# Quarter products inside the second block product of a layernorm, attention and mixture-of-experts kernel

## The chip, the cores and the metric

The kernel runs on one core of one Trainium2 chip. The metric is the device time of one execution in microseconds. The program has five engines that run their own instruction queues in order and meet at semaphores: TensorE (PE, matrix products into PSUM banks), VectorE (DVE), ScalarE (ACT), GpSimd (POOL), and SyncE (SP), which here only issues transfers. POOL and ACT issue some transfers too.

## The reference

All arithmetic is in float32. The input x has 4 rows of 1024 tokens of 1024 channels.

```
xn    = layernorm(x)                                  # over the channels
q, v  = xn @ Wq, xn @ Wv
s_t   = sigmoid(beta) * s_(t-1) + v_t                 # along the tokens, per channel
y     = layernorm(q * s) * ln_g + ln_b
attn  = (y * silu(xn @ Wg)) @ Wo
moe   = for each token the top 8 of 64 experts by softmax(xn @ router.T),
        weights normed over the 8; an expert takes at most 128 tokens:
        (silu(t @ w1.T) * (t @ v1.T)) @ w2
out   = x + attn + moe
```

The change touches only the products with Wv, Wq and Wg, and the norming and turning of the tokens that feed them.

## The kernel before, in words

**Stages.** `attn_and_routing` works through the rows b = 0 to 3 one after the other. In a row the products with Wv and Wq alternate (v unit 0, q unit 0, v unit 1 and so on to q unit 3), then come four gate units with Wg. A unit m makes output channels 128 m to 128 m + 127 and the same 512 further, for all 1024 tokens of the row. Then `Experts` runs the experts and the product with Wo to the end. The experts start at about 1215.9 us of the profile.

**A unit.** A unit is one call of `product`: a product of 2 x 2 blocks in the Winograd form of Strassen's method, with seven block products instead of eight. The left blocks are 512 x 128 pieces of a weight matrix (and sums of them), the right blocks B11, B21, B12, B22 are the normed, transposed tokens (512 channels x 512 tokens) and the sums T1 to T4 of them. `steps` writes the order: slot 0 with B11, slot 1 with B21, slot 5 with T2, slot 4 with T1, slot 3 with T3, slot 6 with B22, slot 2 with T4. The inner function `acc` issues one block product as four matmuls of 128 x 128 by 128 x 512 (L145). Bank "a" gathers slots 0, 5, 3 and 2, bank "b" slot 1, bank "c" slots 4 and 6. In between ACT copies banks to SBUF (L156), and DVE adds them to the results c11 (L168), c22 (L177) and c12 (L180). The seventh product of a unit is left over as `before` and is issued inside the next unit, between its second and third. `late` is a hook for work issued behind the fifth.

**Weights and sums.** `left_sums` makes the four left sums of a unit's weights. In row 0 `weights` loads four pieces of 256 KB through SP, POOL adds (L55 to L58), and a store keeps the 1792 KB in `wsum` (L585); later rows load them from there in one transfer. `right_sums`, called by `sums`, makes T3, T1 (in place of B12), T2 and T4 on DVE (L65, L69, L72, L75).

**Tokens.** Row 0's tokens are normed and turned in `prep_first`; `store` writes them to the DRAM table `rows` (L478, POOL's queue). For row b + 1, `prep(b + 1, h)` takes half of the tokens h in two groups of two 128-token tiles: loads through SP, moments on DVE (L293), root on ACT, reciprocal and norm on DVE (L297), and stores to `rows` through POOL (L441). `load_turned` reads them back through SP in 32-row strips (16 transfers of 128 KB a half), and DVE turns them by 32 x 32 squares into the blocks (L462). The tiles x of two groups have one buffer each. `prep` of the first half is called behind q unit 1, `load_turned` behind q unit 2; of the second half before gate 0 and before gate 3.

**Routing.** `scored` makes the router's logits on TensorE (L487), `route` the choice of eight per token on DVE with the exponent on ACT, and stores to `wtab` (L530). `take` keeps each expert's 128 tokens by 16 rounds of MAX8 (L562) and MATCH_REPLACE (L564) on DVE, spread over the units 0 to 3. `find_spread`, the `late` work of gate 0, makes mean and variance of y by matmuls (L620) and the reciprocal root (L695).

**Order.** The program's order on an engine comes from the scheduler, which keeps dependencies and otherwise places by its own estimates; an instruction given to `keep_in_program_order` stays behind those given before it on its engine. An engine that waits for a semaphore holds everything behind it.

Of the kernel before, what the change touches and what calls it, by code (L numbers as in the profile page):

```python
# [9 lines left out]
F32 = mybir.dt.float32  # L10
I32 = mybir.dt.int32
AF = mybir.ActivationFunctionType
# [5 lines left out]
P = 128  # L18
# [23 lines left out]

NSLOT = 7
NWT = 4

# [33 lines left out]
def load_block(nc, to, w, i, c0, n):  # L79

    nc.sync.dma_start(
        out=to, in_=w[i * SH : (i + 1) * SH, c0 : c0 + n].rearrange("(k p) n -> p k n", p=P)
    )
# [22 lines left out]
class Pools:  # L106
# [17 lines left out]

    def x(self, name):
        return self.three.tile([P, 3, S], F32, tag="x", bufs=2, name=name)

# [9 lines left out]

def steps(nc, pools, lhs, blocks, c11, c12, c22, then, name, begun=None):

    def acc(ps, slot, right, start, stop):
        for k in range(KH):
            nc.tensor.matmul(  # L145
                ps,
                lhsT=lhs[:, slot, k, :],
                rhs=blocks[right][:, k, :],
                start=start and k == 0,
                stop=stop and k == KH - 1,  # L150
                skip_group_check=True,
            )

    def copied(ps, part):
        t = pools.scratch.tile([P, SH], F32, tag="sc", name=f"sc{part}_{name}")
        nc.scalar.copy(t, ps)  # L156
        return t

    a, b = begun if begun else (pools.bank("a", [P, SH], f"pa_{name}"), None)
    if not begun:  # L160
        acc(a, 0, "B11", True, True)
    s1 = copied(a, 1)
    yield
    if not begun:
        b = pools.bank("b", [P, SH], f"pb_{name}")
        acc(b, 1, "B21", True, True)
    yield
    nc.vector.tensor_tensor(c11, b, s1, ALU.add)  # L168
    acc(a, 5, "T2", False, True)
    s2 = copied(a, 2)  # L170
    yield
    c = pools.bank("c", [P, SH], f"pc_{name}")
    acc(c, 4, "T1", True, True)
    s5 = copied(c, 5)
    yield
    acc(a, 3, "T3", False, True)
    nc.vector.tensor_tensor(c22, a, s5, ALU.add)  # L177
    yield
    acc(c, 6, "B22", False, True)
    nc.vector.tensor_tensor(c12, c, s2, ALU.add)  # L180
    yield
    acc(a, 2, "T4", False, True)
    then(a)


def product(nc, pools, lhs, blocks, c11, c12, c22, then, before, name, late=None, begun=None):


    todo = steps(nc, pools, lhs, blocks, c11, c12, c22, then, name, begun)
    next(todo)  # L190
    next(todo)
    if before is not None:
        before()
    for _ in range(3):
        next(todo)
    if late is not None:
        late()
    next(todo)
    return lambda: next(todo, None)
# [3 lines left out]
def kernel(  # L203
# [22 lines left out]
    gated = dram.tile([B, NM, P, 4, KH, P], F32, name="gated")  # L226
    wsum = dram.tile([3, NM, P, NSLOT, KH, P], F32, name="wsum")

    pools = Pools(ctx, tc)
# [4 lines left out]
    attn_and_routing(  # L234
        tc, pools, ident, rows, wtab, gated, wsum, x, (wv, wq, wg), beta, ln_g, ln_b, router, out,
        experts.begin, experts.turn_first,
# [3 lines left out]

def attn_and_routing(
    tc, pools, ident, rows, wtab, gated, wsum, x, wvqg, beta, ln_g, ln_b, router, out, routed,
    turn_first
):
# [68 lines left out]
    def prep_first():  # L313
# [3 lines left out]
        for h in range(2):  # L317
            for i in range(2):
                blocks[f"B{i + 1}{h + 1}"] = pools.block(f"xT_0_{h}_{i}")
        groups = [(pools.y if g > 1 else pools.x)(f"x_0_{g}") for g in range(NM)]  # L320
        tiles = [xs[:, j, :] for xs in groups for j in range(2)]
# [90 lines left out]

    stored = {}

    def prep(b, h):

        groups = stored[b, h] = []
        for g in range(NM // 2):

            xs = pools.x(f"x_{b}_{h}_{g}")  # L420
            mv = small.tile([P, 2, 2], F32, tag="mv", name=f"mv_{b}_{h}_{g}")
            r0 = b * S + h * SH + 2 * g * P
            for j in range(2):
                loaded = nc.sync.dma_start(
                    out=xs[:, j, :], in_=x[r0 + j * P : r0 + (j + 1) * P, :]
                )
                tc.keep_in_program_order(loaded)
                moments(xs[:, j, :], mv[:, j, :], f"{b}_{h}_{g}_{j}")
            rs = small.tile([P, 2], F32, tag="rs", name=f"rs_{b}_{h}_{g}")
            nc.scalar.activation(rs, mv[:, :, 1], AF.Sqrt, bias=eps)  # L430
            nc.vector.reciprocal(rs, rs)
            groups.append((r0, xs, mv, rs))
        for r0, xs, mv, rs in groups:
            for j in range(2):

                to = xs[:, (2, 0)[j], :]
                normed(
                    by_quarter(xs[:, j, :], "k q"), mv[:, j, :], rs[:, j : j + 1],
                    by_quarter(to, "q k"),
                )  # L440
                nc.gpsimd.dma_start(out=rows[r0 + j * P : r0 + (j + 1) * P, :], in_=to)  # L441

    def load_turned(b, h):
# [3 lines left out]
        for i in range(2):  # L447
            blocks[f"B{i + 1}{h + 1}"] = pools.block(f"xT_{b}_{h}_{i}")
        for r0, xs, _, _ in stored[b, h]:
            for j in range(2):  # L450
                from_ = rows[r0 + j * P : r0 + (j + 1) * P, :]
                for q in range(NQ):
                    loaded = nc.sync.dma_start(
                        out=xs[q * Q : (q + 1) * Q, j + 1, :].rearrange("i (r c) -> i r c", r=NQ),
                        in_=from_[:, q * DQ : (q + 1) * DQ].rearrange("(r i) c -> i r c", i=Q),
                    )
                    tc.keep_in_program_order(loaded)
        for g, (_, xs, _, _) in enumerate(stored.pop((b, h))):
            for j in range(2):
                n = 2 * g + j  # L460
                for i in range(2):
                    nc.vector.transpose(  # L462
                        blocks[f"B{i + 1}{h + 1}"][:, :, n * P : (n + 1) * P].rearrange(
                            "p k (r i) -> p k r i", i=Q
                        ),
                        xs[:, j + 1, :].rearrange("p (r k j) -> p k r j", r=NQ, j=Q)[
                            :, i * KH : (i + 1) * KH
                        ],
                    )
# [98 lines left out]
    def sums(b):  # L568
        for _ in right_sums(
# [4 lines left out]
        ):  # L574
            pass

    def weights(b, w, m):
# [8 lines left out]
        else:  # L586
            nc.sync.dma_start(out=t, in_=wsum[w, m])
        return t
# [7 lines left out]
    def batch_row(b, left):  # L596
# [11 lines left out]
        spread = []  # L608
        waiting = []

        def collect_waiting():
# [22 lines left out]
        def states(m, left):  # L634

            lo = line.tile([P, S], F32, tag="line", name=f"lo_{b}_{m}")
            hi = line.tile([P, S], F32, tag="line", name=f"hi_{b}_{m}")

            def then(c21):
                scan(lo, lo, m, 0.0)  # L640
                scan(hi[:, H0], c21, m + KH, 0.0)
                scan(hi[:, H1], hi[:, H1], m + KH, hi[:, SH - 1 : SH])

            left = product(
                nc, pools, weights(b, 0, m), quarters[b],
                lo[:, H0], lo[:, H1], hi[:, H1], then, left, f"v_{b}_{m}", collect_waiting,
                begun.get(0) if b == 0 and m == 0 else None,
            )
            return lo, hi, left

        def queries(m, lo, hi, left):
# [12 lines left out]
            def then(c21):  # L664
# [6 lines left out]
                if m == NM - 1:  # L671
                    collect_waiting()

            left = product(
                nc, pools, weights(b, 1, m), quarters[b],
                y(m, H0), y(m, H1), y(m + KH, H1), then, left, f"q_{b}_{m}", None,
                begun.get(1) if b == 0 and m == 0 else None,
            )
            return left
# [18 lines left out]
        def gates(m, w, left):  # L698
            lo = line.tile([P, S], F32, tag="line", name=f"glo_{b}_{m}")
            hi = line.tile([P, S], F32, tag="line", name=f"ghi_{b}_{m}")  # L700

            def then(c21):
# [4 lines left out]
                for i, (c, gate) in enumerate(((m, lo), (m + KH, hi))):  # L707
# [9 lines left out]
                    for h in range(2):  # L717
# [4 lines left out]
                        )  # L722

            return product(
                nc, pools, w, quarters[b],
                lo[:, H0], lo[:, H1], hi[:, H1], then, left, f"g_{b}_{m}",
                find_spread if m == 0 else None,
            )

        taking = take(b)  # L730
        for m in range(NM):
# [15 lines left out]
            if b + 1 < B:  # L747
                if m == 1:
                    prep(b + 1, 0)
                elif m == 2:  # L750
                    load_turned(b + 1, 0)
# [9 lines left out]
        for m in range(NM):  # L761
            if m == 0 and b + 1 < B:
                prep(b + 1, 1)
            if m == NM - 1 and b + 1 < B:
                load_turned(b + 1, 1)
                logits[b + 1] = by_token(b + 1, scored(b + 1))
                sums(b + 1)
            w = weights(b, 2, m)
            if m == NM - 1 and b == B - 1:
# [79 lines left out]
class Experts:  # L849
# [8 lines left out]
    def load(self, e, n):  # L858
# [13 lines left out]
        if slot not in self.slots:  # L872
            t = (pools.x if e == 0 and n < 2 else pools.y)(f"w{n}_{e}")
            self.slots[slot] = t.rearrange("p a b -> p (a b)")
# [422 lines left out]
```

## Time and profile before

| | us |
|---|---|
| median of 3 runs (lowest, highest) | 2531.57 (2531.47, 2532.62) |
| the profiled execution | 2531.94 |
| its span in the profile | 2530.2 |

| stretch of the span, us | what | PE busy | DVE busy | POOL busy |
|---|---|---|---|---|
| 0 to 215.09 | row 0, v and q | 211.55 | 154.44 | 75.24 |
| 215.09 to 322.12 | row 0, gates | 106.51 | 79.23 | 38.49 |
| 322.12 to 1215.9 | rows 1 to 3 | 893.76 | 558.33 | 145.96 |
| 1215.9 to 2530.2 | experts, output | 1305.63 | 937.03 | 506.50 |

The second table comes from the profile's view by stretches. The page gives busy time for each engine; a float32 matmul leaves two records in it and in the timelines. In the timelines a row has its start, its length, engine, line and operation, the tiles written and read, the number of records, and in brackets how long the engine had been idle and what ended that. In the waits a row has the total, the count and the longest. Lines L... are those of the kernel before.

### The profile page before, as it was taken

The page shows a single profiled execution, that of the slowest core. Times are in us where ns is not written, and L with a number is a line of the kernel's source. Part 1 is how long each engine was busy: PE and PEld are TensorE (multiplying, and loading weights), DVE is VectorE, ACT ScalarE, POOL GpSimd, SP SyncE. Part 2 cuts the span into 40 slices and gives each one's busy share as a digit, 9 for nine tenths or more (in the row PEclk, how much of TensorE's full clock was granted, in tenths as well). Part 3 has the DMA queues.
Part 4 walks back from the last instruction along what each step waited for, and adds up shares of the span by engine and source line. Part 5 has one row for each costly group of instructions (what it writes and reads, how often), then busy time and mean ns, then how long its engine had stood idle before and what let it go on. Part 6 is the DMA issues. An engine that isn't in the chain of part 4 may idle for free. (4 is left out here: it accounts for less than half of the span.)

```text
span 2530.2 us, 23616 instructions
## 1 busy us (share of the span) xinstructions
PE 2517.4 (99%) x8253; PEld 1107.4 (44%) x8253; DVE 1729.0 (68%) x2178; ACT 821.7 (32%) x1930; POOL 766.2 (30%) x629
## 2 busy tenths in 40 slices
PE   9999999999999999999999999999999999999998
PEld 5444444444444444444444444444444444444443
DVE  7857659474684747447786767677676768677674
ACT  3112211131111311022253535444454545444452
POOL 0453301201122010231342434344433434344421
PEclk9999999999999999999999999999999999999999
DMA  5665625543344532145799999999999999999995
GB/s 187 256 199 206 203 80 180 186 142 108 133 154 178 166 142 91 59 172 182 279 350 290 309 315 322 311 297 323 308 321 295 313 311 324 309 300 318 312 319 138
DMA packets 122503, 593.80 MB, mean 235 GB/s; under 512 B 15872, under 2 KB 52736, under 8 KB 89360
## 3 DMA queue, kind: packets, MB, share of 16 engines
q1 hardware_dynamic: 81776, 449.08, 48.2%
q0 software_dynamic: 40176, 143.20, 22.0%
q8 instruction: 65, 1.06, 0.2%
q14 instruction: 54, 0.44, 0.0%
q10 hardware_dynamic: 432, 0.01, 0.0%
HBM read 484.19 MB, written 124.81 MB: 241 GB/s over the span
## 5 line engine op out<-in xcount | busy, mean ns | idle before, releaser
L889 POOL DMA_INDIRECT xg<-rows,tables x256 | 290.7, 1136 | 299.0 <-DVE xgT L937 218.7
L976 DVE TENSOR_TENSOR t<-w 128x1536 f32<-128x1536 f32 x128 | 224.3, 1752 | 225.5 <-PE hC L995 222.2
L1087 POOL DMA_INDIRECT out_dram<-ys,tables x64 | 124.5, 1945 | 384.3 <-issue 139.3
L145 PE MATMUL pa_g<-xT,w 128*128 128x512 f32 x512 | 230.9, 594 | 0.5 <-ACT sc_g L156 0.5
L145 PE MATMUL pa_q<-xT,w 128*128 128x512 f32 x480 | 216.4, 593 | 0.0
L145 PE MATMUL pa_v<-xT,w 128*128 128x512 f32 x480 | 215.8, 592 | 0.0
L995 PE MATMUL hC<-t,s 128*64 128x384 f32 x512 | 177.3, 489 | 0.0
L995 PE MATMUL hC<-w,s 128*64 128x384 f32 x512 | 177.3, 490 | 0.0
L1083 PE MATMUL hD<-w,act 128*128 128x512 f32 x384 | 175.3, 592 | 0.6 <-ACT act L1072 0.6
L995 PE MATMUL hA<-w,s 128*64 128x384 f32 x512 | 175.6, 486 | 0.0
L995 PE MATMUL hB<-w,xgT 128*64 128x384 f32 x512 | 175.6, 486 | 0.0
L995 PE MATMUL hA<-w,xgT 128*64 128x384 f32 x512 | 175.6, 486 | 0.0
L995 PE MATMUL hD<-t,s 128*64 128x384 f32 x512 | 175.6, 486 | 0.0
L1083 PE MATMUL hT<-w,act 128*128 128x512 f32 x384 | 175.3, 592 | 0.0
L145 PE MATMUL pa_o<-wo_T,gated 128*128 128x512 f32 x384 | 174.2, 596 | 0.0
L145 PEld LDWEIGHTS pa_g<-xT,w 128*128 128x128 f32 x512 | 96.3, 190 | 123.7 <-issue 123.4
L145 PEld LDWEIGHTS pa_q<-xT,w 128*128 128x128 f32 x480 | 91.1, 190 | 114.5 <-issue 113.0
L145 PEld LDWEIGHTS pa_v<-xT,w 128*128 128x128 f32 x480 | 90.9, 190 | 112.8 <-issue 111.9
L719 POOL DMA_DIRECT2D gated<-y x64 | 48.0, 756 | 302.0 <-DVE y L714 287.7
L1061 ACT COPY act<-s 32x96 f32<-32x96 f32 x480 | 129.0, 269 | 7.0
L1061 ACT COPY act<-t 32x96 f32<-32x96 f32 x480 | 128.9, 269 | 6.0
L145 PE MATMUL pc_g<-xT,w 128*128 128x512 f32 x256 | 115.5, 594 | 0.0
(250 smaller groups left out, 4437.2 us busy)
## 6 DMA issues: line engine op xcount, KB each, us to landing
w<-in_w_dram SPq DMA_DIRECT2D x128, 1536.0 KB, 8.2
w<-in_v_dram SPq DMA_DIRECT2D x64, 1536.0 KB, 8.7
w<-wsum SPq DMA_DIRECT2D x36, 1792.0 KB, 7.4
wsum<-w POOLq DMA_DIRECT2D x12, 1792.0 KB, 6.2
x<-in_x_dram SPq DMA_DIRECT2D x32, 512.0 KB, 9.3
rows<-x POOLq DMA_DIRECT2D x32, 512.0 KB, 4.3
gated<-y POOLq DMA_DIRECT2D x64, 256.0 KB, 5.4
gated<-gated SPq DMA_DIRECT2D x16, 1024.0 KB, 8.4
```

Source lines behind the costliest of these rows:

```text
L145: nc.tensor.matmul(ps, lhsT=lhs[:, slot, k, :], rhs=blocks[right][:, k, :], start=start and k == 0, stop=stop and k == KH - 1, skip_group_ ...
L719: nc.gpsimd.dma_start(out=gated[b, :, :, slot, m, :].rearrange("u p j -> p u j"), in_=yc[:, h * SH : (h + 1) * SH].rearrange("p (u j) -> p ...
L889: nc.gpsimd.indirect_dma_start(out=self.xg[:, e % 2 * NQ + r, :], out_offset=None, in_=self.rows.rearrange("n (q c) -> (n q) c", q=NQ), in ...
L976: self.nc.vector.tensor_tensor(to, a, b, ALU.subtract)
L995: nc.tensor.matmul(bank[half], lhsT=a[:, ks[k], :], rhs=b[:, ks[k], :], start=(k == 0), stop=(k == len(ks) - 1), tile_position=(0, half.st ...
L1061: self.nc.scalar.copy(self.hT(e)[q * Q : (q + 1) * Q, :, r * Q : (r + 1) * Q], split[r * Q : (r + 1) * Q, :, q, :],)
L1083: nc.tensor.matmul(ps, lhsT=hT[:, j, :], rhs=w2[:, j, cols], start=(j == 0), stop=(j == KF - 1))
L1087: nc.gpsimd.indirect_dma_start(out=self.out, out_offset=bass.IndirectOffsetOnAxis(ap=self.idx[:, e : e + 1], axis=0), in_=ys, in_offset=No ...
```

## The change

The block product of slot 1 (B21) is cut once more in rows 1 to 3. Two units m and m + 1 (m even) share the right block B21, and their two left blocks together make a 512 x 256 matrix. `inner_steps` multiplies it with B21 by seven quarter products in the same form: left quarters of 256 x 128, right quarters of 256 channels x 256 tokens, each product two matmuls of 128 x 128 by 128 x 256. The results of unit m go into its c11 (`top`), those of unit m + 1 into that unit's c11 (`bottom`), which is allocated ahead; c11 is then added from SBUF. The quarter products are issued in three pieces, in unit m only: ia, ic and ib where slot 1 was; three behind the left-over seventh product; one before slot 4. They use bank "b" twice and bank "t" once. Unit m + 1 has no slot 1.

Five left quarters per pair are read from a new DRAM table `wsum2` (640 KB a pair) with the even unit's weights, into a tile "inside". `inner_weights` makes the table in row 0 at gates 0 to 2, for one weight matrix each: a 512 KB load, four adds on POOL and two stores per pair. The right sums of the quarters are made on DVE by `right_sums` behind the outer ones, with B21's quarters, four of 128 x 512 per row.

The second x tile becomes this "inside" tile (tag x2), so that the groups of next tokens share a single x buffer. `prep` handles one group at a time, as `late` work of q units 0 and 1 and of gates 0 and 1; `load_turned` brings both groups through the one buffer, the second behind the first's transposes. The loads of weights in rows 1 and 2, and of v and q in row 3, are kept in program order.

```diff
+NIN = 5
+KQ, SQ = KH // 2, SH // 2
...
-        return self.three.tile([P, 3, S], F32, tag="x", bufs=2, name=name)
+    def x(self, name, second=False):
+        return self.three.tile([P, 3, S], F32, tag="x2" if second else "x", bufs=1, name=name)
...
+def inner_steps(nc, pools, lhs, more, blocks, top, bottom, name):
+    lefts = [lhs[:, 1, 0:KQ], lhs[:, 1, KQ:KH]] + [more[:, i] for i in range(NIN)]
+
+    def acc(ps, slot, right, start=False):
+        for k in range(KQ):
+            nc.tensor.matmul(
+                ps,
+                lhsT=lefts[slot][:, k, :],
+                rhs=blocks[right][:, k, :],
...
+    q0, q1 = slice(0, SQ), slice(SQ, SH)
+    a, c, b = (
+        pools.bank(tag, [P, SH], f"{n}_{name}")[:, q0]
+        for tag, n in (("b", "ia"), ("b", "ic"), ("t", "ib"))
+    )
+    acc(a, 0, "B11", True)
+    nc.scalar.copy(top[:, q0], a)
+    acc(c, 4, "T1", True)
+    nc.scalar.copy(bottom[:, q1], c)
+    acc(b, 1, "B21", True)
+    add(top[:, q0], b)
+    yield
+    acc(a, 5, "T2")
+    nc.scalar.copy(top[:, q1], a)
+    acc(c, 6, "B22")
+    add(top[:, q1], c)
+    acc(a, 3, "T3")
+    add(bottom[:, q1], a)
+    yield
+    acc(a, 2, "T4")
+    nc.scalar.copy(bottom[:, q0], a)
+    yield
...
     s1 = copied(a, 1)
     yield
-    if not begun:
+    if inner is not None:
+        inner = iter(inner)
+        next(inner, None)
+    elif not begun:
         b = pools.bank("b", [P, SH], f"pb_{name}")
         acc(b, 1, "B21", True, True)
     yield
+    if inner is not None:
+        next(inner, None)
+        b = c11
     nc.vector.tensor_tensor(c11, b, s1, ALU.add)
     acc(a, 5, "T2", False, True)
     s2 = copied(a, 2)
     yield
+    if inner is not None:
+        next(inner, None)
     c = pools.bank("c", [P, SH], f"pc_{name}")
...
-    def prep(b, h):
...
-        for g in range(NM // 2):
...
+    def prep(b, h, g):
...
+        xs = pools.x(f"x_{b}_{h}_{g}")
...
-        for r0, xs, _, _ in stored[b, h]:
+        for g in range(NM // 2):
+            xs = pools.x(f"xq_{b}_{h}_{g}")
...
+        if b > 0:
+            (t,) = inside
+            b21 = quarters[b]["B21"]
...
+            for _ in right_sums(nc.vector, blocks, lambda n: free.pop()):
+                pass
+            quarters[b]["inner"] = blocks
...
+    def inner_weights(w, pair):
...
+        tc.keep_in_program_order(load_block(nc, a, wvqg[w], i, o * SH + 2 * pair * P, 2 * P))
...
+        add = nc.gpsimd.tensor_tensor
+        add(s1, a21, a22, ALU.add)
+        add(s2, s1, a11, ALU.subtract)
+        add(s3, a11, a21, ALU.subtract)
+        add(s4, a12, s2, ALU.subtract)
+        nc.gpsimd.dma_start(out=wsum2[w, pair, :, 0], in_=a22)
+        nc.gpsimd.dma_start(out=wsum2[w, pair, :, 1:], in_=to)
...
-            nc.sync.dma_start(out=t, in_=wsum[w, m])
+            pin = tc.keep_in_program_order if b < B - 1 or w < 2 else lambda ins: None
+            pin(nc.sync.dma_start(out=t, in_=wsum[w, m]))
+            if m % 2 == 0:
+                pin(nc.sync.dma_start(out=inner_lefts(), in_=wsum2[w, m // 2]))
...
-                y(m, H0), y(m, H1), y(m + KH, H1), then, left, f"q_{b}_{m}", None,
+                y(m, H0), y(m, H1), y(m + KH, H1), then, left, f"q_{b}_{m}",
+                (lambda: prep(b + 1, 0, m)) if m < 2 else None,
                 begun.get(1) if b == 0 and m == 0 else None,
+                inner(m, w, y(m, H0), "q", lambda: y(m + 1, H0)),
...
+            def late():
+                if m == 0:
+                    find_spread()
+                prep(b + 1, 1, m)
...
-                if m == 1:
-                    prep(b + 1, 0)
-                elif m == 2:
+                if m == 2:
                     load_turned(b + 1, 0)
...
         for m in range(NM):
-            if m == 0 and b + 1 < B:
-                prep(b + 1, 1)
+            w = weights(b, 2, m)
             if m == NM - 1 and b + 1 < B:
                 load_turned(b + 1, 1)
                 logits[b + 1] = by_token(b + 1, scored(b + 1))
                 sums(b + 1)
-            w = weights(b, 2, m)
+            if b == 0 and m < NM - 1:
+                for pair in range(NM // 2):
+                    inner_weights(m, pair)
```

## The prediction

> **What bounds the kernel now.** I read the page's first two parts, then the engines' waits, then the groups kept apart by shape, then the timelines of the stages the diff touches. The page first:
>
> ```profile
> PE 2517.4 (99%) x8253; PEld 1107.4 (44%) x8253; DVE 1729.0 (68%) x2178; ACT 821.7 (32%) x1930; POOL 766.2 (30%) x629
> ...
> PE   9999999999999999999999999999999999999998
> ...
> PEclk9999999999999999999999999999999999999999
> ```
>
> TensorE is the bound in every slice, at an undisturbed clock. Its waits:
>
> ```profile
> PE warm L254 <- DVE best L280: 2.1, 1, 2.1
> ...
> PE pa_g L145 <- ACT sc_g L156: 0.5, 1, 0.5
> ```
>
> Some 4.7 us are idle in all, none of it in rows 1 to 3. So a matmul that goes is worth its whole time, and every wait that the change puts in front of TensorE is a loss of its whole length: no slack absorbs it. What one matmul costs by width:
>
> ```profile
> 26.64 1.89 PE L355 MATMUL pb<-xT,w 128*128 128x256 f32 x8
> 28.37 1.89 PE L355 MATMUL pa<-xT,w 128*128 128x256 f32 x8
> 30.09 1.89 PE L355 MATMUL pb<-xT,w 128*128 128x256 f32 x8
> ...
> 432.42 3.60 PE L145 MATMUL pc_v<-xT,w 128*128 128x512 f32 x8
> 435.85 3.60 PE L145 MATMUL pa_v<-xT,w 128*128 128x512 f32 x8
> ```
>
> A row is four matmuls (two records each). From start to start, four of 512 columns take 435.85 - 432.42 = 3.43 us, four of 256 columns 28.37 - 26.64 = 1.73 and 30.09 - 28.37 = 1.72.
>
> **What goes.** In rows 1 to 3 a pair of units loses two B21 products, 2 x 3.43 = 6.87 us, and gains seven products of two matmuls of 256 columns, 7 x 1.725 / 2 = 6.04. That is 0.83 us a pair; 3 rows x 3 weight matrices x 2 pairs = 18 pairs: **-15.0 us**. [...] The rows above, in this kernel's own type and with a new weight load for each matmul, show half (1.725 of 3.43); the loads of weights (190 ns a record in the page's groups) still fit under a record of 216. I take the row.
>
> **What is added beside TensorE.** Per pair four ACT copies and three DVE adds of 128x256, for one c11 add that reads SBUF instead of PSUM. A 128x512 copy is 585 ns (L156), an add 684 (L168): half the width lies between 0.3 and 0.6 each. DVE is 68% busy, so the work has room on average; only its place in the in-order queue counts. Per row, four right sums of 128x512 (0.68 each, by the row of L55) also go to DVE. Row 0 gains six 512 KB loads, 24 POOL adds of 128x256 and stores; rows 1 to 3 gain 18 loads of 640 KB. Between nothing and their landing time, they cost nothing where they come before their user: a 1792 KB load of wsum takes 7.4 us to land and units are 24 us apart. The x and second x buffers still reach the experts' first weights by gate 3; I book 0, ends -1 and +1.
>
> **What is moved, and what waits.** I laid the new program order against these rows. Each is a wait of TensorE, which I give as central value and ends.
>
> 1. Row 0, second v unit, step T2: **+6.5 (0 to 10)**. Before:
>
> ```profile
> 63.65 1.53 POOL L530 DMA_DIRECT2D wtab<-sh  x2 [2.58 <-DVE sh L527]
> 65.18 3.73 POOL L478 DMA_DIRECT2D rows<-x  x7
> ...
> 70.87 1.27 POOL L55 TENSOR_TENSOR w<-w 128x512 f32<-128x512 f32 x1
> 72.22 1.26 POOL L56 TENSOR_TENSOR w<-w 128x512 f32<-128x512 f32 x1
> 73.44 2.24 POOL L57 TENSOR_TENSOR w<-w 128x512 f32<-128x512 f32 x1
> 75.65 1.26 POOL L58 TENSOR_TENSOR w<-w 128x512 f32<-128x512 f32 x1
> ```
>
> The left sums stand on POOL behind the row stores and are done at 76.9; TensorE takes slot 5 at 81.11. After, the first x tiles of row 1 are loaded behind the first q unit. With one x buffer that load waits for the store of row 0's first group: the first of the seven at 65.18, landing 4.3 later (the median of these stores), about 69.5. I take 5 and 8 us for the two landings (the window's median is 6.8): 74.5 and 77.5. DVE, in order, waits there with bn_stats (4 x 0.6), then cur (1.3), y's product (1.95), the reciprocal after ACT's root (table load 1.28), a MAX8 1.35 and two norms (0.8 each): norms near 83.5 and 85.7. On POOL the two stores of these tiles (0.56) now stand before and after L55's add, so slot 5 (L56) is ready at 86.3 + 1.3 = 87.6, against 81.1.
>
> 2. Row 0, gate 2, T4 of gate 1: **+2.5 (0 to 6)**. POOL and SP build the quarter weights here, so the second half's last x tiles load some 4 us later. DVE idles in bn_stats and does 3 us of moments before this reciprocal:
>
> ```profile
> 254.97 6.54 DVE L695 RECIPROCAL rstd<-rstd 128x1024 f32<-128x1024 f32 x1
> ...
> 269.67 0.68 DVE L177 TENSOR_TENSOR ghi<-pa_g,sc_g 128x512 f32<-128x512 f32 x1
> ```
>
> The add that frees the bank moves from 270.4 to about 275.5; T4 wants it at 273.2.
>
> 3. The three row starts: **+4.5 (0 to 9)**. The second quarter product ("ic") needs the inner right sum T1', which stands on DVE behind the outer ones; the outer T1 overwrites B12 and so waits for the router's matmuls (7.0 us in the timeline of row 0), which the new order puts behind gate 3's T3. Counted from gate 3's start in row 0: six products (A, B21, gate 2's T4, T2, T1, T3) end at 6 x 3.43 = 20.6, the router at 27.6. DVE then does three outer sums (2.39 apart, by the timeline of L69 to L75: 314.34, 316.74, 319.13), three adds of 0.6 and T1' itself (0.68): 27.6 + 7.2 + 1.8 + 0.7 = 37.3. TensorE has the token transposes (0.4), A of the new unit and B22 of gate 3 (6.9), "ia" and half of "ib" (1.3) before it: 36.2. So 1.1 us by the sum, and with half a microsecond for the hand-over and a reduction of 0.6 near it in row 0 I take 1.9 + 1.3 + 1.3. The first pair's DVE adds wait behind it, and c11 after these, which T4 does not need.
>
> 4. First q unit, rows 1 and 2: **+1 (0 to 5)**. Its copies stand behind the routing's exp on ACT (a table load of 1.28 with it), its adds on DVE behind the early moments, where DVE now waits for an x load. Where that load lands in time the queue runs about 0.5 over, each.
>
> 5. Third v unit, rows 1 and 2: **+2.4 (0 to 7)**. The last quarter product waits for a DVE add behind take's rounds:
>
> ```profile
> 435.08 1.35 DVE L562 MAX8 best<-cur 64x8 f32<-64x1152 f32 x1
> 436.47 0.22 DVE L559 COPY cur<-best 64x128 f32<-64x128 f32 x1
> ```
>
> Here the last of take's 16 rounds (about 2.75 us each) ends one product after the third v unit has begun. From cur on, I count 57.65 us of DVE work ahead of that add, and 56.55 us of TensorE: 1.2 each with the hand-over. Row 3, without next tokens, has none: it has 8 x 0.6 of moments and 4 x 0.8 of norms less.
>
> 6. Gate 1, rows 1 and 2: **+2.6 (0 to 6)**. The variance matmul (L620) stands in TensorE's queue among gate 1's products and waits for sum2, now behind the moments (four of 0.6) of the second group, whose load lands some 28 us into the gates, after the first group's stores: sum2 is ready at 37.4 from gate 0's start, TensorE at 36.2.
>
> The sum is +19.5. From the profiled execution's 2531.94 (1.7 over its span; the median of the runs is 2531.57, 0.4 lower): 2531.9 - 15.0 + 19.5 = **2536.4**.
>
> **Rivals.** *The covers hold (faster).* Items 2, 4, 5 and 6 are each 1 to 2 us over a cover of tens of us, within what DVE's durations vary (L714: 1.28 alone, 2.28 beside POOL). If they go, 1 at 4 and 3 at 3 stay: 2531.9 - 15.0 + 7 = 2524. For it: no DVE wait reaches TensorE in rows 1 to 3 now. Against: 1 follows from a buffer and two in-order queues, not from a close race. It decides when the x tiles land by 70.
>
> *The SP queue holds the weights back (slower).* The single x buffer makes SP wait, between two groups of eight loads, for DVE's transposes of the first group, and the fourth v unit's weights are pinned behind. Before, 16 issues took 10 to 13 us unbroken. I find the weights landing 6 us before use. If take's MAX8 rounds hold the transposes longer than that, say by 11, three rows lose 5 each: 2536.4 + 15 = 2551. It decides when the fourth v unit's first matmul waits for wsum.
>
> *It doesn't do what it says.* If switches between narrow and wide products cost one record (0.2 us) at each of three places a pair, 18 x 0.6 = 11 of the 15 are lost: 2547. The rows at 26.64 to 31.91 show no such gap between banks; a switch of width they barely show.
>
> **How the numbers follow.** Forecast as worked out, 0.50; covers hold, 0.25; SP queue, 0.15; no gain, 0.10. A change under 0.2%, 5.1 us, can hardly be told from none. The forecast's own range, with the items' ends partly compensating, is 2530 to 2543; it straddles 2536.6, so half of its chance is "slower" and half "same". Faster (below 2526.5): most of the second case, 0.24. Same: 0.26. Slower: 0.50. Range for 8 in 10: 2521 to 2551.
>
> **What would show it.** Matmuls of 128x256 in rows 1 to 3 at 1.72 us per eight records prove the saving; PE busy near 2502. The waits of PE should name POOL's w for the second v unit (6.5), DVE's inside at three row starts (1 to 2 each), DVE's ghi at gate 2 of row 0, and sum2 for var. I am wrong if PE's waits sum to less than 10 us or more than 30, or if a DMA of wsum is the longest.

## The result and the profile after

The changed kernel takes 2541.22 us (median of 7 runs, 2537.66 to 2541.82), the kernel before 2531.56 in runs beside it: 9.7 us more, a ratio of 1.0035 with a 95% interval of 1.0023 to 1.0046. That is slower by more than the measurement's uncertainty. The profiled execution has a span of 2539.4 us, against 2530.2.

The first part of the page of the changed kernel, and the longest of TensorE's waits in it (total, times, longest, in us). From here on, lines L... are those of the kernel that each view belongs to.

```profile
PE 2510.5 (99%) x8469; PEld 1149.5 (45%) x8469; DVE 1766.2 (70%) x2244; ACT 852.8 (34%) x2006; POOL 778.4 (31%) x665
```

```profile
PE pc_v L193 <- POOL w L59: 7.7, 1, 7.7
PE ia_v L149 <- DVE lo L159: 3.7, 3, 1.5
PE pa_g L193 <- DVE ghi L233: 3.2, 1, 3.2
PE warm L313 <- DVE best L339: 2.1, 1, 2.1
PE var L744 <- DVE sum L820: 1.9, 1, 1.9
PE ic_v L149 <- DVE xT L73: 1.1, 2, 0.5
PE pa_v L193 <- POOL w L60: 0.6, 1, 0.6
```

All of TensorE's waits were 4.7 us before; now they are 22.1. The share of busy time still reads 99%: it hides the loss. There is a second oddity: PE busy fell by only 6.9 us, while the quarter products should have taken 15.0 out. Most of the missing 8.1, namely 5.1, is a slower clock, which counts as busy time. The largest piece of it is in the second v unit of row 0. Here is TensorE's timeline there, and then the view by stretches around it (length, busy time and records of PE, PEld, DVE, ACT and POOL, then the granted clock, the DMA share and GB/s):

```profile
78.25 3.60 PE L193 MATMUL pa<-xT,w 128*128 128x512 f32 x8
89.59 2.08 PE L193 MATMUL pc_v<-xT,w 128*128 128x512 f32 x2 [7.74 <-POOL w L59]
92.29 5.82 PE L193 MATMUL pa_v<-xT,w 128*128 128x512 f32 x8 [0.62 <-POOL w L60]
97.95 2.74 PE L193 MATMUL pc_v<-xT,w 128*128 128x512 f32 x6
100.52 3.60 PE L193 MATMUL pa_v<-xT,w 128*128 128x512 f32 x8
```

```profile
72.00:81.00 9.00, 9.00 (x22) 3.98 (x22) 1.99 (x4) 0.00 (x0) 0.00 (x0) 1.00 1.01 366
89.50:91.50 2.00, 1.91 (x2) 0.50 (x2) 1.97 (x3) 0.00 (x0) 1.14 (x3) 0.50 0.28 111
97.50:99.50 2.00, 2.00 (x6) 0.95 (x5) 1.97 (x4) 0.58 (x1) 1.92 (x3) 1.00 1.02 436
```

After the gap of 7.7 us the granted clock is 0.50. The 16 records from 89.59 to 100.52 take 10.93 us, of which 0.8 is the second wait; at full clock they take 6.87. The slow clock costs 3.3 us that no list of waits shows, because TensorE counts as busy. The gap of 3.2 us at gate 2 of row 0 is followed by the same: the granted clock is 0.50 from 292.30 to 294.30, and 16 records from 290.30 to 298.97 take 8.67 us instead of 6.87, 1.8 more.

The saving is there. This is TensorE in the third v unit of row 1:

```profile
446.11 1.03 PE L149 MATMUL ia_v<-inside 128*128 128x256 f32 x4
446.97 1.03 PE L149 MATMUL ic_v<-xT,inside 128*128 128x256 f32 x4
447.83 1.03 PE L149 MATMUL ia_v<-inside 128*128 128x256 f32 x4
448.70 3.60 PE L193 MATMUL pa_v<-xT,w 128*128 128x512 f32 x8
453.39 1.13 PE L149 MATMUL ia_v<-inside 128*128 128x256 f32 x4 [1.10 <-DVE lo L159]
```

A quarter product of two matmuls takes 0.86 us from start to start, with no gap where the width changes: the wide product ahead of 446.11 starts at 442.67, 3.44 before, and the narrow one at 447.83 is followed by the wide one after 0.87. The last row also shows how a wait is read: 453.39 - 448.70 = 4.69 is the product's 3.43 and 1.26 more, while the bracket says 1.10. The ends are modelled, and a wait is some 0.16 longer than listed; I call that its edge.

**The sum up to the experts.** They begin at 1226.60 instead of 1215.85, 10.75 later. Saved -15.0; new waits in row 0 13.5 (7.74, 0.62, 1.95, 3.22) and in rows 1 to 3 5.3; one wait of before (0.5, at gate 0) gone; slow clock 5.1; ten waits' edges 1.6; a start that was 0.6 later at 78 us. Together 10.6. The experts themselves took the same within 0.2 us, and the end after TensorE's last product was 1.3 us shorter.

**Why TensorE waits at 89.6.** The timelines of DVE and of POOL:

```profile
78.75 1.29 DVE L352 BATCH_NORM_STATS2 st<-x 128x6 f32<-128x512 f32 x2 [9.55 <-DMA x<-in_x_dram]
...
81.25 1.29 DVE L352 BATCH_NORM_STATS2 st<-x 128x6 f32<-128x512 f32 x2 [0.51 <-DMA x<-in_x_dram]
...
86.46 0.78 DVE L356 TENSOR_SCALAR x<-x,mv,rs 128x1024 f32<-128x1024 f32 x1
```

```profile
87.53 0.67 POOL L494 DMA_DIRECT2D rows<-x  x1 [16.15 <-DVE x L356]
88.27 1.26 POOL L59 TENSOR_TENSOR w<-w 128x512 f32<-128x512 f32 x1
90.38 0.56 POOL L494 DMA_DIRECT2D rows<-x  x1 [0.84 <-DVE x L356]
90.95 1.28 POOL L60 TENSOR_TENSOR w<-w 128x512 f32<-128x512 f32 x1
```

Three queues in order hand the wait on. DVE stands 9.6 us before the moments of tiles whose load came late, POOL stands 16 us before the store of their normed rows, and behind that store is the left sum that TensorE wants.

### The profile page after: what moved, and what is told of

The parts are those of the page before. It is cut to its first block, busy times and chain, and to the rows that moved or that the text cites. A ratio compares the mean times of both kernels' runs of the same rounds, so it can differ in the third digit from the quotient of the medians.

```text
span 2539.4 us, 24283 instructions
## 1 busy us (share of the span) xinstructions
PE 2510.5 (99%) x8469; PEld 1149.5 (45%) x8469; DVE 1766.2 (70%) x2244; ACT 852.8 (34%) x2006; POOL 778.4 (31%) x665
## 3 DMA queue, kind: packets, MB, share of 16 engines
q0 software_dynamic: 41328, 147.13, 22.1%
## 5 line engine op out<-in xcount | busy, mean ns | idle before, releaser
L1024 POOL DMA_INDIRECT xg<-rows,tables x256 | 285.2, 1114 | 308.6 <-DVE xgT L1072 200.8
L193 PE MATMUL pc_v<-xT,w 128*128 128x512 f32 x256 | 116.3, 596 | 7.7 <-POOL w L59 7.7
```

The lines of the kernel that those rows point to most:

```text
L193: nc.tensor.matmul(ps, lhsT=lhs[:, slot, k, :], rhs=blocks[right][:, k, :], start=start and k == 0, stop=stop and k == KH - 1, skip_group_ ...
L1024: nc.gpsimd.indirect_dma_start(out=self.xg[:, e % 2 * NQ + r, :], out_offset=None, in_=self.rows.rearrange("n (q c) -> (n q) c", q=NQ), in ...
```

## The experiments

Each kernel is compared by its distance to the kernel before, run beside it on the same chip; for the changed kernel this is +9.7.

**1. The left sums ahead of the stores** (row 0 only)

```diff
+            if b == 0 and m == 0:
+                early[1] = weights(b, 0, 1)
+            prep(b + 1, 0, m)
```

The four adds of these sums, and the row stores of the first group behind them, are kept in program order on POOL.

> The changed kernel, but in row 0 the left sums of the second v unit stand on POOL ahead of the two row stores of the next row's first tiles; the early norming and DVE's wait for the x load stay. Theory (POOL's queue carries the wait: the sums are held behind stores that wait for DVE's norms): TensorE's waits in that unit (7.7 + 0.6 us) go, and with them the slow clock after them, which I read as 3.4 us; about 2541.2 - 11.8 = 2529.4. Rival (DVE's in-order wait of 9.6 us for the x load is itself the loss): the wait turns up one or two steps later, where TensorE needs a DVE add to free a bank; gain under 4 us, 2537 to 2541.

2531.79 us, -0.9 to before (2532.69), ratio 0.9997 (0.9989 to 1.0005). The 7.7 and 0.6 are gone, and 10.6 us of the time with them. POOL's order carried this wait, but it was not all that could hold the unit. One row of the waits, its place in the timeline, and ACT ahead of it:

```profile
PE pa_v L193 <- ACT sc_v L204: 2.3, 1, 2.3
```

```profile
83.60 5.37 PE L193 MATMUL pa_v<-xT,w 128*128 128x512 f32 x8 [2.29 <-ACT sc_v L204]
```

```profile
82.69 0.29 ACT L485 ACTIVATE rs<-mv,eps 128x2 f32<-128x2 f32 x1 [13.27 <-DVE mv L353]
82.89 0.57 ACT L204 COPY sc_v<-pa_v 128x512 f32<-128x512 f32 x1
```

ACT stands 13.3 us before the root of the same moments, and the copy that frees the bank stands behind it. So ACT is a fourth queue that the late x load holds. The clock fell here after a gap of only 2.29 us: it is 0.52 from 86 to 88 us, and eight records take 5.2 us (83.60 to 88.81) instead of 3.43. The waits at sum2 and at gate 2 were 2.7 and 1.7 us in this run, after 1.9 and 3.2.

**2. The second half's x loads ahead of the quarter tables** (row 0)

```diff
         for m in range(NM):
             w = weights(b, 2, m)
+            if b == 0 and m < 2:
+                prep(b + 1, 1, m)
```

> The changed kernel, but in row 0 the loads of the second half's next tokens stand on SP ahead of the loads for the quarter weights, one gate each. Theory (the x load comes late because SP waits for the quarter table's stores): the waits of the variance product (1.9) and at gate 2 (3.2, with 1.8 of slow clock after it) go; about 2541.2 - 7 = 2534. Rival (the moments, wherever they stand, delay the reciprocal): both waits stay within 1 us; 2540 to 2542. Second rival (SP's wait is only moved): TensorE waits for the gate weights instead.

2550.2 us, +17.5, ratio 1.0066 (1.0052 to 1.0080). A miss. The wait at gate 2 went, the one for sum2 grew to 2.9, and a new one of 3.6 came at the router's products, which need the turned tokens, again with a slow clock behind it (32 records in 8.78 instead of 7.09). Only part of the new wait is that the tokens came later: SP began to read the rows back at 301.1 us instead of 298.8, and these products began 1.1 us later than in the changed kernel (331.03 instead of 329.96). The rest is TensorE, which was there 2.6 us earlier, since it had not waited at gate 2. The profiled execution took 2544.7 and the median is 5.5 above it, so the profile does not show the whole loss.

**3. No quarter products**

```diff
         def inner(m, lhs, top, name, bottom):
-            if b == 0:
-                return None
...
+            return None
```

> The changed kernel with everything kept but the quarter products: rows 1 to 3 make the second block product whole again; the quarter table, its loads and the inner right sums stay and are not used. Theory (the quarters save 15.0 us of TensorE and cost 4.8 us of waits for ia and ic): 2541.2 + 15.0 - 4.8 = 2551. Rival (the quarters save little because switches of width cost a record): 2541 or less.

2548.46 us, +15.8, ratio 1.0061 (1.0047 to 1.0075). The inner right sums still put T1' in place of one quarter of B21, so this kernel multiplies other data in the second product; its work is that of the whole products. Busy time of PE is 2523.4, 12.9 above the changed kernel. Without the quarters the waits for ia and ic are gone, and at gate 2 1.1 us are waited instead of 3.2, with no slow clock after. It is 6.1 us slower than the changed kernel. From the 15.0 go 4.8 of waits, 0.8 of edges and 3.9 at gate 2 (2.1 of wait, 1.8 of clock), while other waits grew by 2.2 (sum2 0.7, ACT copies 0.9, a load of the experts 0.6). That leaves 7.7; the profiled executions' spans differ by 7.5. The quarters themselves pay; what came with them costs more.

**4. The last quarter product behind slot 4's**

```diff
-    if inner is not None:
-        next(inner, None)
     c = pools.bank("c", [P, SH], f"pc_{name}")
     acc(c, 4, "T1", True, True)
     s5 = copied(c, 5)
+    if inner is not None:
+        next(inner, None)
```

> The changed kernel, but the last quarter product stands behind slot 4's product instead of ahead of it. Theory (it waits for one DVE add that is about 1.1 to 1.5 us late, and 3.4 us of other product cover that): the three waits of ia for lo (3.7 us) go; 2537.3. Rival (the add is late since DVE is behind as a whole): the wait comes back at a later bank; 2540 to 2542.

2546.97 us, +14.3, ratio 1.0053 (1.0039 to 1.0067). The waits of ia are gone, but the waits of the variance's product went from one to three:

```profile
PE var L744 <- DVE sum L820: 9.2, 3, 3.9
```

The rival, in another place than it named. The two new waits, 3.3 and 3.9 us, each have a slow clock behind them. After the first the variance's four records take 1.90 us instead of 1.01 and the next four 3.58 instead of 1.72. For the second it is read from TensorE's busy time: 2512.7 us, 8.0 above run 10, which has no slow records; of these 8.0, the gaps of 7.7 and 3.3 us account for 6.0. The scheduler set DVE's order anew: in row 1 the moments of the second group now stand ahead of all the steps to sum2 and wait there for their load. In the changed kernel they stand behind the first of these steps and wait 0.4 us. DVE's timeline of this run:

```profile
551.60 1.29 DVE L352 BATCH_NORM_STATS2 st<-x 128x6 f32<-128x512 f32 x2 [7.18 <-DMA x<-in_x_dram]
```

**5. Row 0's early norming one unit later**

```diff
-                (lambda: prep(b + 1, 0, m)) if m < 2 else None,
+                (lambda: prep(b + 1, 0, m - (b == 0))) if (b == 0) <= m < 2 else None,
...
+                if b == 0 and m == 1:
+                    prep(b + 1, 0, 1)
```

> The changed kernel, but in row 0 the first two groups of next tokens are normed one unit later (behind the second q unit and after it), as late as before the change; rows 1 and 2 stay. The first run of this study left a wait of 2.3 us in the second v unit, for an ACT copy behind ACT's root of the early moments. Theory (all of the loss in that unit comes from norming behind the first q unit): no wait and no slow clock there; 11.9 us off the changed kernel, about 2529.5, some 2 us below the run with the sums first. Rival (the single x buffer only moves it): the wait turns up in the third v unit or at load_turned; 2535 or more.

2528.22 us, -3.5 to before (2531.68), ratio 0.9986 (0.9980 to 0.9993). There is no wait in the second v unit of row 0, and the ones that the rival named, in the third v unit or for the turned rows, did not come there either. The waits for sum2 and at gate 2 stay, with 2.7 and 2.9 us. This one placement in row 0 made the difference between slower and faster.

**6. The tables behind the next gate's weights** (row 0)

```diff
-            if b == 0 and m < NM - 1:
-                for pair in range(NM // 2):
-                    inner_weights(m, pair)
...
             left = gates(m, w, left)
+            if b == 0 and m < NM - 1:
+                ahead_w.append(weights(b, 2, m + 1))
+                for pair in range(NM // 2):
+                    inner_weights(m, pair)
```

> The changed kernel, but in row 0 the quarter table of a weight matrix is made after its gate is issued, behind the next gate's weights, so that SP has the second group's x load behind one table instead of two. Theory (DVE's 4.7 us of waiting for that load is what makes the reciprocal late): the load lands near 265 instead of 269.5, the waits for sum2 (1.9) and at gate 2 (3.2, and 1.8 of slow clock) shrink to under 2 us together; about 2536. Rival (the moments ahead of the reciprocal are enough): both stay, 2540 to 2542; or the rows' way back is late and the router's products wait as in the run with the loads first, 2545.

2560.86 us, +29.2, ratio 1.0112 (1.0097 to 1.0128). The theory failed: the wait at gate 2 went, but the one for sum2 grew to 5.1. The last rival held, much larger than it said:

```profile
PE lg L541 <- DVE xT L516: 16.9, 1, 16.9
```

SP reads the rows back (16 transfers) behind the third table's loads, which wait for stores. These now begin at 308.8 us instead of 272.9, and the reading back at 324.0 instead of 298.8.

**7 and 8. The gap, and the gap filled.** The first puts slot 4's product ahead of slot 5's in the second v unit of row 0, as a base; the second adds to it nine matmuls (NFILL) into an unused bank, ordered behind the product before the gap and ahead of slot 4's. First the edit of both, then what only the second adds:

```diff
     nc.vector.tensor_tensor(c11, b, s1, ALU.add)
+    if name == "v_0_1":
+        c = pools.bank("c", [P, SH], f"pc_{name}")
+        acc(c, 4, "T1", True, True)
+        s5 = copied(c, 5)
```

```diff
+    for _ in range(NFILL):
+        nc.tensor.matmul(
+            bank, lhsT=FILL["ident"], rhs=blocks["B11"][:, 0, :], start=True, stop=True
+        )
...
+    if name == "v_0_1":
+        fill(nc, pools, blocks)
```

> The changed kernel with slot 4's product ahead of slot 5's in the second v unit of row 0, as base for the next run. TensorE waits 7.7 us for the first left sum there, and then the whole of slots 4 and 5 is issued in one piece. Theory (after a gap of some 8 us TensorE runs at half clock for a while): the first 16 records behind the gap take some 10.3 us instead of 6.9; total within 1.5 us of the changed kernel. Rival (the slow records are an effect of the second wait or of the interleaving): 6.9 us.

> The run before it, with nine matmuls of 128x512 into an unused bank put into the gap (9 x 0.86 = 7.7 us), so that TensorE isn't idle; the left sum comes no earlier. They add to the work and change no result. Theory (the idle gap itself lowers the clock): the granted clock stays at 1, the 16 records take 6.9 us, and the kernel is 3.4 us faster than the run before it, although it does more. Rival (the slow records come from POOL and DVE at work beside, or from the wait's release): they take 10.3 us as before and the time is the same.

The first took 2537.30 us (+5.6, ratio 1.0025, 1.0014 to 1.0036), the second 2540.05 (+8.4, 1.0035, 1.0023 to 1.0047). First the base, then the filled kernel, in TensorE's timeline:

```profile
89.17 6.59 PE L193 MATMUL pc_v<-xT,w 128*128 128x512 f32 x8 [7.72 <-POOL w L59]
95.59 3.60 PE L193 MATMUL pa_v<-xT,w 128*128 128x512 f32 x8
99.03 1.02 PE L193 MATMUL pc_v<-xT,w 128*128 128x512 f32 x2
```

```profile
81.44 7.89 PE L204 MATMUL fill<-xT,ident 128*128 128x512 f32 x18
89.27 3.70 PE L219 MATMUL pc_v<-xT,w 128*128 128x512 f32 x8
92.81 3.60 PE L219 MATMUL pa_v<-xT,w 128*128 128x512 f32 x8
96.24 1.02 PE L219 MATMUL pc_v<-xT,w 128*128 128x512 f32 x2
...
112.30 3.70 PE L219 MATMUL pa_v<-xT,w 128*128 128x512 f32 x8 [2.08 <-DVE hi L267]
138.26 3.70 PE L219 MATMUL pa_q<-xT,w 128*128 128x512 f32 x8 [1.66 <-DVE y L267]
```

The same 16 records take 99.03 - 89.17 = 9.9 us behind an idle gap and 96.24 - 89.27 = 7.0 behind a filled one, with POOL and DVE at the same work beside (from 80 to 102 us POOL is busy for 13.6 and 13.5 us, DVE for 21.3 in both); the granted clock is 0.50 from 88 to 94 us in the first and 1.00 from 80 to 102 in the second. Here the gap is what lowers the clock. The base took somewhat less than the expected 10.3, and its total lies 4 us nearer to the kernel before than I had said. The gain in time did not come: the medians stand the other way, with ranges that overlap (2536.4 to 2540.6 and 2537.5 to 2542.5), so which of the two is faster stays open. TensorE, 2.9 us earlier, then waits 2.1 and 1.7 us for two DVE adds. The first of them in DVE's timeline, with the row up to which both runs agree; base, then filled:

```profile
102.93 0.63 DVE L357 BATCH_NORM_STATS2 st<-x 128x6 f32<-128x512 f32 x1
103.66 0.69 DVE L238 TENSOR_TENSOR hi<-pa_v,sc_v 128x512 f32<-128x512 f32 x1
```

```profile
103.03 0.63 DVE L389 BATCH_NORM_STATS2 st<-x 128x6 f32<-128x512 f32 x1
...
111.58 0.66 DVE L267 TENSOR_TENSOR hi<-pa_v,sc_v 128x512 f32<-128x512 f32 x1
```

Up to here DVE runs at the same times in both, within 0.1 us. Then, in the filled kernel, the scheduler put 8 us of take's rounds and of the norming ahead of the add, although its product was done earlier. So the two runs differ in DVE's order too, and what the filled gap alone is worth in total time is not shown.

**9. Two raw tables, and the last moments behind sum2** (on top of 5, row 0)

```diff
-        a = t[:, 0:n].rearrange("p (k n) -> p k n", k=KH)
+        a = t[:, 2 * pair * n : (2 * pair + 1) * n].rearrange("p (k n) -> p k n", k=KH)
...
+                tc.keep_in_program_order if (b, h, g) == (1, 1, 1) else lambda ins: None,
...
+            summed = nc.vector.scalar_tensor_tensor(sum2, off, 2.0, sum2, ALU.mult, ALU.add)
+            if b == 0:
+                tc.keep_in_program_order(summed)
```

The first added line gives each raw table its own third of the tile; the others keep the moments of the last group behind sum2.

> The run with the later norming in row 0 (2528.2), and besides in row 0: the raw weights of a gate's second quarter table have their own third of the tile, so that SP doesn't wait for the first table's store; and the moments of the last group of next tokens stand on DVE behind sum2. Theory (what holds T4 at gate 2 is DVE waiting 4.4 us for an x load that SP issued late, ahead of the reciprocal): the wait for ghi (2.9) and its slow clock (1.8) go, the one for sum2 (2.7) stays: about 2523.5. Rival (DVE has simply too much work there): the wait for ghi stays over 2 us, 2527 or more.

2528.58 us, -3.0 to before (2531.58), ratio 0.9985 (0.9978 to 0.9992); its 21 runs lie between 2524.1 and 2532.0. The waits for ghi and for sum2 are both gone, more than expected, but the router's products wait 3.8 us for turned tokens, with 1.7 us of slow clock. No gain over 5 in the median.

**10. Besides, y less the mean behind sum2** (on top of 9, row 0)

```diff
-                        nc.vector.tensor_tensor(yc, yc, mean, ALU.subtract)
+                        less = nc.vector.tensor_tensor(yc, yc, mean, ALU.subtract)
+                        if b == 0:
+                            tc.keep_in_program_order(less)
```

> The run before it, and in row 0 y less the mean (128x1024, 1.2 to 1.7 us each) also stands behind sum2 in DVE's order; in the run with the later norming three of them lay between the steps of sum2. Theory (they are the 2.7 us): no wait for sum2, about 2521. Rival (what is put off comes due at gates 2 and 3 or at row 1's start): new waits for DVE there, 2523 or more.

2523.88 us (2522.22 to 2524.35), -7.7, ratio 0.9968 (0.9957 to 0.9980): faster than both kernels. Its waits of a microsecond or more:

```profile
PE ia_v L149 <- DVE lo L159: 3.8, 3, 1.5
PE warm L313 <- DVE best L339: 2.1, 1, 2.1
PE ic_v L149 <- DVE xT L73: 1.1, 2, 0.5
PE var L747 <- DVE sum L823: 1.0, 1, 1.0
```

The gain is not at sum2, where the theory had it. Its wait, gone in run 9, is back with 1.0 us: sum2 is ready 2.5 us earlier (247.4 instead of 249.9), but the scheduler also put the variance's product earlier into TensorE's queue. What goes is run 9's wait at the router's products: the turned tokens are ready at 311.5 instead of 314.3. SP took 14.7 us to read the rows back instead of 16.2; why is not shown. Nothing that was put off came due. After the warm-up matmuls TensorE has no wait over 1.51 us up to the experts, and none is followed by slow records.

**11. The last quarter behind slot 4's in the third v unit alone** (on top of 9)

```diff
+    late_last = name[0] == "v" and name[-1] == "2"
```

> The run with two tables, and the last quarter product behind slot 4's in the third v unit alone (rows 1 to 3), not in all units as in the earlier run. Theory (the add is late there alone, by less than a product's 3.4 us, and the waits of the earlier run came from the other units): the three waits of ia (3.8 us) go and none takes their place; 3.8 below the run with two tables. Rival (every move of this step changes DVE's order at gate 0): waits for sum2 in rows 1 and 2 as in the earlier run, no gain or a loss.

2534.73 us, +3.2, ratio 1.0011 (1.0003 to 1.0019). Again the rival: the waits of ia go, and sum2 is waited for by 3.4 us in row 1 and 3.9 in row 2, each with slow records behind (the first four in 2.0 us instead of 1.1). As in run 4, the moments stand ahead of all the steps to sum2 and wait there for their load, 7.3 us in row 1. An order pinned on DVE, as in run 10 for row 0, was not tried in these rows.

## Why the prediction was right or wrong

The direction was right: 2536.4 forecast, 2541.2 measured, within the range. Of the sum, -15.0 and +19.5, the first term held and the second was too small: listed waits grew by 17.4 us, but each has an edge, and the slow clock behind two of them adds 5.1. That the new waits (18.8) come so near to the forecast 19.5 is luck: items 1, 2 and 5 were too small, items 3, 4 and 6 too large.

- **What goes.** Held: 0.86 us a quarter product, no loss at changes of width. The rows of 256 columns from before the change were the right ones to take: a record takes 216 ns at 256 columns and 429 at 512 here too, about half. The rival "It doesn't do what it says" is out.
- **Item 1** had the right queue and the wrong size. Forecast 6.5, measured 8.4 and 3.3 of slow clock. The step that failed: "I take 5 and 8 us for the two landings". The loads were issued from 69.2 on, as worked out (69.5), but DVE could begin at 78.75 and 81.25, where the sum had 74.5 and 77.5. The profile page's median for these loads, 9.3, would have given 78.8 for the first; I took 5 and 8, around the window's 6.8. So slot 5's sum was ready at 92.2 instead of 87.6; part of that TensorE covered with two records of slot 4, and it came 0.6 later itself. The experiment with the sums first shows that POOL's order is the path, and that ACT holds a second one behind it.
- **Item 2**: forecast 2.5, measured 3.2 and 1.8 of slow clock. The place and the cause held: runs 9 and 10 undo it in row 0.
- **Item 3**: forecast 4.5, measured 0.54 each for T1' in rows 2 and 3, none for it in row 1, and 0.5 for an ACT copy there. The sum had given 1.1 a row, and what I put on top for the hand-over was not there.
- **Item 4**: forecast 1, nothing measured. **Item 5**: forecast 2.4 in two rows; 3.7 in all three (1.10, 1.10, 1.49). That row 3 "has none" was wrong: there, too, take's rounds fill DVE without a pause, and the last MAX8 (1.35 us, at 1044.35) stands right before the add. The moments and norms, which row 3 lacks, did not decide it. **Item 6**: forecast 2.6 in rows 1 and 2, none there; 1.9 in row 0, where I had not looked.
- **The rivals.** "The covers hold" did not occur: items 2 and 5 came, and so did a wait for sum2. Its sign, x tiles landed by 70, was missed by 9 us. Experiment 5 comes near its 2524 with 2528.2, but by another way: there item 1 is gone and the covers still fail. "The SP queue holds the weights back" did not occur with the fourth v unit's weights: no wait for wsum stands among TensorE's waits. But SP's in-order waits made the turned rows late in run 6, and in part in run 2.
- **The term that was missing** is the clock. "a loss of its whole length" was said of a wait; in these runs a long wait cost more than its length. Behind 7.74 us the granted clock was 0.50 and 3.3 us were lost besides, behind 3.22 us it was 0.50 and 1.8 were lost. Every gap of 2.9 us and more in these runs, after the warm-up, was followed by slow records. The clock also fell after 2.29 us in experiment 1, and it did not after 2.71 at that kernel's variance product (four records in 1.01 us, as without a gap). An estimate from these runs, where gaps of 2.9 us and more lost 1.7 to 3.7 us by their records, and only one of eleven between 1.9 and 2.8 us lost any: item 1, at 6.5, would have been some 8 to 10, and item 2, at 2.5, perhaps nothing more.

## What to carry to other kernels

When the bounding engine is 99% busy, an edit that saves its work can be decided, as here by one wait of 7.74 us, by the in-order queues that feed it: follow each moved load through every engine that will stand before its data (here DVE, then ACT and POOL), and ask what is queued behind. Take a transfer's landing from the profile page's median unless there is a reason for less. Price a gap in TensorE at its length and at the slow clock behind it: in these runs another 1.7 to 3.7 us, by the records, for gaps of 2.9 us and more. Then let the place decide: moving one step of row 0 turned +9.7 us into -3.5, and three more edits there turned that into -7.7. An edit also makes the scheduler order other queues anew (runs 4, 8, 10 and 11), so see in the trace what else moved before you call the edit the cause.

## What the runs showed of the hardware

Filling the gap of 7.7 us with useless products kept the clock (1.00 instead of 0.50, and 2.9 us less over the next 16 records). No gain in time could be seen, but DVE's order had changed as well, so that stays open. A wait in the profile is some 0.16 us longer from start to start than its bracket says (1.26 instead of 1.10 in the third v unit of row 1, 7.91 instead of 7.74 in the second of row 0). And a gap of a given length doesn't always lower the clock: 2.29 us did, 2.71 did not, in the same execution. Of the eleven gaps between 1.9 and 2.8 us in the profiled executions, after the warm-up and up to the experts, that one alone was followed by a lower clock; of the 18 from 2.9 us on (2.90 to 16.91), all were.
